# A two-layer graph network on one core: longer rests in the update chain, ten shared row buffers, full-array products and one activation table

## The chip, the cores and the metric

The kernel runs on one core of a Trainium2 chip. A core has engines that run side by side, each with its own stream of instructions: PE (TensorE, matrix products), DVE (VectorE), ACT (ScalarE), POOL (GpSimd) and SP (SyncE, which here only queues DMA transfers). They wait for one another through semaphores. The metric is the device time of one execution in microseconds (us). Three executions of the kernel before took 3070.16, 3073.55 and 3084.93 us; the median is 3073.55. One more execution was recorded by the hardware profiler, and took 3064.87 us.

## The reference

There are 6250 nodes with 256 features, and 106250 edges (50000 pairs in both directions and a loop at every node), sorted by destination. Each edge has one of two types. The first layer:

```python
msgs = zeros_like(S)                          # S = x[src]
for r in range(2):                            # edge_nn: two relu layers with the same weights
    msgs = where((rel == r)[:, None], edge_nn(S, W_rel[r], b_rel[r]), msgs)
agg = segment_sum(msgs, dst)
i, f, g, o = split(agg @ W_ih.T + b_ih + b_hh, 4)
c = sigmoid(i) * tanh(g);  hn = sigmoid(o) * tanh(c)
h = relu(hn @ W1.T + b1);  h = relu(h @ W2.T + b2);  out = h @ W3.T + b3
x = layernorm(x + out)
```

The second is an attention layer with four heads of 64 features, with a maximum over the edges that enter each node:

```python
h = (x @ W).reshape(n, 4, 64)
e = leaky_relu(a_src[src] + a_dst[dst], 0.2)  # a_src = sum(h * att_src), a_dst likewise
ex = exp(e - segment_max(e, dst)[dst])
alpha = ex / segment_sum(ex, dst)[dst]
o = segment_sum(h[src] * alpha[..., None], dst) + bias
y = relu(layernorm(o + x) * ln_gamma + ln_beta)
x = layernorm(x + y)
```

All data is float32.

## The kernel before

**Messages.** A message depends on the source node and the edge type alone, so the messages of all nodes are computed once for both types, split in three bfloat16 parts (768 numbers of 2 bytes a row), and written to the table `parts0` in DRAM. Beside it the kernel makes the indices of the rows that each edge needs (`idx0` for layer 0, `idx1` for layer 1), and for each edge the place of its destination in its window (`slot`).

**Tiles, windows, groups, pairs.** 128 edges are a tile; there are 831 tiles. Seven tiles are a window (119 windows), whose destinations lie in 64 consecutive nodes; the tile after the seventh may still hold edges of the window, so a window is summed over eight tiles (`tiles_of(w)[1]`), and a tile at a border is used by two windows. Two windows are a group of 128 node slots (60 groups), and two groups a pair, except the last four groups, which stand alone.

**The order of the work** is written by hand (`tc.manual_schedule()`): each engine runs its instructions in the order of the code. One loop over the tiles per layer issues one gather a step (L1057, an indirect DMA on POOL's queue that fetches 128 rows by index), then the matmuls that are due, and then `run.step()`. The class `Steps` (L1065) holds chains, written as generators: at each step every chain that is due runs on to its next `yield n`, and rests n steps. So a chain's stages are spread between the gathers and the sum's matmuls of later tiles.

**Layer 0.** Gathers go to 20 buffers of one tile (`g0`). Four steps (`LAG`) after its gather, a tile is added to its group's sum in PSUM by three matmuls, one for each bfloat16 part, with a one-hot matrix of the destinations as the stationary operand (`sum0`, L1337). When a group is full, the chain `turn` copies the sum (L1177) and transposes it on PE (L1181); when a pair is full, the chain `update` runs: the gates (L1214 on PE, L1222 on ACT, sigmoid and tanh), the cell (L1227 to L1233), three linear layers (L1237 to L1257), the residual and layernorm (L1260 to L1276), transposes (L1282), and the product with the attention weights (L1294). It writes the rows of layer 1 (264 numbers, of which 260 are stored) to `rows1` (L1304) and the values needed later to `kept`, and fills `node3`, which holds the node's part of the attention logits as three bfloat16 parts.

**Layer 1.** Gathers go to seven buffers of one window each (`G`, seven tiles). The chain `ahead` (L1406) loads the destinations of the pair's edges, makes a transposed one-hot matrix, and spreads the nodes' logits to the edges by small products (L1449: 64 rows, 8 columns, three parts summed in PSUM), copied by ACT at L1460. The chain `weights` (L1463) takes the segment maxima with scans along the edges and ends in `ex`, the exponentials; it waits in `while late` until the windows of the pair before have been taken up. `weighted` (L1514) makes a window's one-hot matrix and multiplies its gathered rows by `ex` (L1529, tile `gw`); the multiplication is the last use of the row buffer `G`. `sum1` (L1617) adds tile after tile to the group's sum (L1633, in float32). The chain `finish` (L1536) divides, adds the loop's part, and does both layernorms with Sqrt on ACT (L1576) and a reciprocal on DVE (L1580).

A gather into a buffer waits until the buffer's last reader is done: the sum's matmuls in layer 0, the multiplication into `gw` in layer 1. ACT holds one set of function tables at a time; where the next function is of another set, a table load (`ACT_TABLE_LOAD`) stands ahead of it.

Of the kernel before, what the change touches and what calls it, by code (L numbers as in the profile page):

```python
# [44 lines left out]
H = 4  # L45
# [652 lines left out]
def gnn_kernel(  # L698
# [66 lines left out]
    with (  # L765
# [15 lines left out]
        with (  # L781
# [110 lines left out]
            nc.vector.tensor_sub(slot[:, : NW - 1, WT], after, lows[:, : NW - 1])  # L892
# [99 lines left out]
def fast(  # L992
# [103 lines left out]

    iops = ctx.enter_context(tc.tile_pool(name="iops", bufs=1, space=PSUM))
    iota8 = iops.tile([P, WT + 1, SLOTS], F32, name="iota8")
    for j in range(WT + 1):
        nc.scalar.copy(iota8[:, j, :], iota_f[:, :SLOTS])  # L1100
    keep = ctx.enter_context(tc.tile_pool(name="keep", bufs=1))
    node3 = keep.tile([P, NG, 3, 2 * H], BF16, name="node3")
    loop = keep.tile([P, NG, H], F32, name="loop")
    eps_c = keep.tile([P, 1], F32, name="eps_c")
    nc.vector.memset(eps_c, EPS)
    ctx.enter_context(tc.manual_schedule())

    def one_hot(to, w, nj):
        nc.vector.tensor_tensor(  # L1109
            to[:, :nj, :],  # L1110
            iota8[:, :nj, :],
            slot[:, w, :nj, None].to_broadcast([P, nj, SLOTS]),
            op=OP.is_equal,
        )


    with (
# [31 lines left out]
        nc.sync.dma_start(W3T_s, W3T)  # L1149
        zero = l0w.tile([(NP + P - N) // 2, 2 * HA], F32, name="zero")  # L1150
# [20 lines left out]
        def turn(g, i, ps, aT):  # L1171
# [6 lines left out]
            yield 1  # L1178
# [9 lines left out]
        def update(groups, aT):  # L1188
            cols = len(groups) * P
# [11 lines left out]
            yield 2  # L1201
            hn = up.tile([P, 2, 2 * P], F32, name="fhn")
            cells = []
            for m in range(2):
                gate = {}
                for name, part, func in (
# [14 lines left out]
                    gate[name] = up.tile([P, 2 * P], F32, name="f" + name, bufs=4)  # L1221
# [3 lines left out]
                    yield 1  # L1225
                cell = gate["gg"][:, :cols]
                nc.vector.tensor_mul(cell, cell, gate["gi"][:, :cols])  # L1227
                cells.append((cell, gate["go"][:, :cols]))
            for m, (cell, go) in enumerate(cells):
                nc.scalar.activation(cell, cell, AF.Tanh)  # L1230
            yield 1
            for m, (cell, go) in enumerate(cells):
                nc.vector.tensor_mul(hn[:, m, :cols], cell, go)  # L1233
            yield 1
# [7 lines left out]
            yield 2  # L1242
# [4 lines left out]
            yield 2  # L1247
# [4 lines left out]
            for i, g in enumerate(groups):  # L1252
# [6 lines left out]
                nc.vector.tensor_add(xn[u, i, :], xn[u, i, :], b3r[u, :])  # L1259
# [4 lines left out]
                yield 1  # L1264
            r = rstd[:, : len(groups)]
            nc.scalar.activation(r, mv[:, : len(groups), 1], AF.Sqrt, bias=eps_c)
            yield 2
            nc.vector.reciprocal(r, r)
            for i, g in enumerate(groups):
# [5 lines left out]
            yield 1  # L1275
            hs = []  # L1276
# [12 lines left out]
            yield 1  # L1289
            for i, g in enumerate(groups):  # L1290
# [6 lines left out]
                hr = up.tile([P, D + 2 * H], F32, name="hr")  # L1297
                nc.scalar.copy(hr[u, :], ph[u, :])
                nc.scalar.copy(keep3[u, i, 2, :], ph[u, :D])
                yield 1  # L1300
                for w in windows_of(g):
# [3 lines left out]
                    else:  # L1305
# [5 lines left out]
                        )  # L1311
                nc.sync.dma_start(kept[g, u, :], keep3[u, i, :, :].rearrange("p c f -> p (c f)"))

                nd = up.tile([P, 2, H], F32, name="nd")
                left = up.tile([P, 2, H], F32, name="left")
                nc.vector.tensor_copy(nd[u, 0, :], hr[u, HA : HA + H])
# [3 lines left out]
                n3 = [node3[u, g, c, :].rearrange("p (a h) -> p a h", a=2) for c in range(3)]  # L1320
# [4 lines left out]
                nc.vector.tensor_sub(n3[2], left[u, :, :], n3[1])  # L1325

        got, ohs, sums, turned = {}, {}, {}, {}
# [25 lines left out]
        for t in range(EC + LAG):  # L1353
            if t < EC:
                got[t] = ep.tile([P, 3 * D], BF16, name="g0", bufs=20)
                gather(got[t], parts0, idx0[:, t : t + 1])
                if t % WT == 0:
                    w = t // WT
                    ohs[w] = ep.tile([P, WT + 1, SLOTS], BF16, name="oh0")
                    one_hot(ohs[w], w, len(tiles_of(w)[1]))  # L1360
# [9 lines left out]
    with (  # L1370
        tc.tile_pool(name="fl1", bufs=1) as l1,
# [6 lines left out]
        vec = l1.tile([P, 2, D], F32, name="fvec")  # L1378
        for k, v in enumerate((gamma, beta)):
            nc.sync.dma_start(vec[:, k, :], rows(v, D))  # L1380
        slot_p = l1.tile([P, 1], F32, name="slot_p")
# [362 lines left out]
```

## Time and profile before

| quantity | value |
|---|---|
| median of three executions | 3073.55 us |
| profiled execution | 3064.87 us |
| its span, first to last instruction | 3063.1 us |
| PE busy (x instructions) | 1868.3 us (61%), x9984 |
| DVE busy | 1256.6 us (41%), x3394 |
| ACT busy | 767.3 us (25%), x1829 |
| POOL busy | 1583.2 us (52%), x1674 |
| stages: start / layer-0 gathers / gap / layer-1 gathers / end | 196 / 1234 / 46 / 1501 / 86 us |
| gathers of layer 0 and of layer 1, L1057 | 831 and 831, 949 and 951 ns each |
| fps matmuls of layer 0, L1337 | 2847, 433.8 us |
| fps matmuls of layer 1, L1633 | 1898 records, 650.7 us |
| pn products, L1449 | 2847, 100.8 us |
| ACT table loads, L1576, L1548, L1222 | 60, 58 and 31, 1283 ns each |

How to read it: busy times are of instructions that do work; waits, branches and the issue of a transfer are not in them. A row of the profile such as "L1529 DVE TENSOR_TENSOR gw<-G,exE 128x1792 f32 x118" is a group of instructions by line, engine, operation and tiles. "[10.19 <-DVE gw L1529]" is idle time of the engine ahead of an instruction, and what ended it. "issue" is time for which the profile shows no wait. Granted clock is the TensorE clock that was allowed, as a share of the full one.

### The profile page before, as it was taken

Reading aid. Unit: us, or ns where it says so; the run is one execution under the profiler, and the core shown is the slowest. Engines: PE = TensorE matmul, PEld = TensorE weight load, DVE = VectorE, ACT = ScalarE, POOL = GpSimd, SP = SyncE. Lnnn points to the kernel's source line nnn. Section 1 sums busy time; section 2 is a strip of 40 time slices with the busy share of each in tenths; the row PEclk is TensorE's granted clock in tenths of the full one; section 3 lists DMA queues with packets and bytes.
Section 4 is the critical chain, followed back from the end, with each engine's and each line's share of the span. In section 5 each row is a group of like instructions: output and inputs, shape, how many; then the busy total and the mean of one; then the engine's idle time right before and its main releaser. Section 6 shows DMA issues by size and latency. Waiting matters only on the chain. (4 is left out here: it accounts for less than half of the span.)

```text
span 3063.1 us, 31458 instructions
## 1 busy us (share of the span) xinstructions
PE 1868.3 (61%) x9984; PEld 1092.3 (36%) x9984; DVE 1256.6 (41%) x3394; ACT 767.3 (25%) x1829; POOL 1583.2 (52%) x1674
## 2 busy tenths in 40 slices
PE   8956777776777676778145554545454545454544
PEld 5644444444444444445122222222222222222222
DVE  6531222222222222223135555554555454545556
ACT  5631222222222222223012222222222222222223
POOL 0036666666666666664545554555455545454540
PEclk9977778878878888888566666666666766666667
DMA  4455555555555555554423434343434343434331
GB/s 152 155 166 145 158 164 164 164 166 162 157 168 165 164 171 162 159 167 136 119 71 98 114 101 110 100 113 100 110 100 113 100 111 98 112 97 115 97 103 32
DMA packets 183539, 395.17 MB, mean 129 GB/s; under 512 B 51925, under 2 KB 91800, under 8 KB 183362
## 3 DMA queue, kind: packets, MB, share of 16 engines
q0 software_dynamic: 93168, 274.27, 32.9%
q1 hardware_dynamic: 88993, 118.00, 12.5%
q8 instruction: 80, 1.31, 0.2%
q10 hardware_dynamic: 1200, 0.79, 0.1%
q14 instruction: 98, 0.79, 0.1%
HBM read 333.63 MB, written 59.30 MB: 128 GB/s over the span
## 5 line engine op out<-in xcount | busy, mean ns | idle before, releaser
L1057 POOL DMA_INDIRECT G<-rows,fidx x831 | 790.1, 951 | 714.8 <-DVE gw L1529 463.0
L1057 POOL DMA_INDIRECT g<-parts,fidx x831 | 788.7, 949 | 638.4 <-DVE zero L1151 193.9
L1633 PE MATMUL fps<-gw,oh 128*64 128x264 f32 x1898 | 650.7, 502 | 248.1 <-DVE gw L1529 166.4
L1337 PE MATMUL fps<-g,oh 128*64 128x256 bf16 x2847 | 433.8, 311 | 69.8 <-DVE oh L1109 25.8
L1633 PEld LDWEIGHTS fps<-gw,oh 128*64 128x64 f32 x1898 | 294.2, 173 | 498.1 <-issue 371.0
L1337 PEld LDWEIGHTS <-oh 128*64 128x64 bf16 x2847 | 275.4, 121 | 248.2 <-issue 188.3
L1529 DVE TENSOR_TENSOR gw<-G,exE 128x1792 f32<-128x1792 f32 (+1 forms) x237 | 278.3, 1215 | 90.8 <-ACT gw L1521 75.6
L1214 PE MATMUL fpg<-faT,fWihT 128*128 128x256 f32 (+1 forms) x768 | 250.3, 456 | 71.8 <-issue 61.4
L1109 DVE TENSOR_TENSOR oh<-iota,fslot 128x512 bf16<-128x512 f32 (+1 forms) x238 | 161.7, 680 | 252.2 <-remote 120.5
L1449 PE MATMUL pn<-node,ohT 64*128 64x8 bf16 x2847 | 100.8, 166 | 234.6 <-issue 180.6
L1214 PEld LDWEIGHTS fpg<-faT,fWihT 128*128 128x128 f32 x768 | 151.5, 225 | 135.8 <-issue 102.3
L1449 PEld LDWEIGHTS <-ohT 64*128 64x128 bf16 x2847 | 70.9, 100 | 347.2 <-issue 337.0
L1471 PE MATMUL turn<-fident,e 128*128 128x128 f32 (+2 forms) x32 | 14.9, 465 | 247.6 <-issue 132.0
L1227 DVE TENSOR_TENSOR fgg<-fgg,fgi 128x256 f32<-128x256 f32 (+1 forms) x64 | 26.3, 410 | 292.7 <-issue 175.9
L1576 ACT ACTIVATE frs<-fmv,eps_c 128x1 f32<-128x1 f32 x120 | 35.4, 295 | 424.6 <-issue 173.6
L1460 ACT COPY of<-pn 128x64 f32<-128x64 f32 (+1 forms) x119 | 18.9, 210 | 396.7 <-remote 311.5
L1260 DVE TENSOR_TENSOR keep<-fpg,fxn 128x256 f32<-128x256 f32 (+1 forms) x60 | 25.4, 424 | 222.4 <-PE fps L1337 109.6
L1294 PE MATMUL fpg<-Wx,fyT 128*128 128x264 f32 (+1 forms) x240 | 93.3, 525 | 22.6 <-ACT fyT L1286 12.0
L1584 ACT ACTIVATE fy<-fy,frs 128x256 f32<-128x256 f32 x120 | 71.9, 600 | 121.7 <-DVE frs L1581 100.6
L1184 DVE COPY faT<-fpg 128x256 f32<-128x256 f32 x60 | 24.5, 409 | 182.5 <-remote 98.9
L1471 PEld LDWEIGHTS turn<-fident,e 128*128 128x128 f32 (+2 forms) x32 | 5.6, 174 | 261.7 <-issue 139.0
L934 PE MATMUL fph<-fxc,fWrT 128*128 128x512 f32 (+1 forms) x208 | 89.2, 578 | 0.6 <-ACT fhT L941 0.3
(178 smaller groups left out, 2166.4 us busy)
## 6 DMA issues: line engine op xcount, KB each, us to landing
kept<-keep SPq DMA_DIRECT2D x59, 384.0 KB
k<-kept SPq DMA_DIRECT2D x59, 384.0 KB
parts<-ms SPq DMA_DIRECT2D x49, 384.0 KB
g<-parts,fidx POOLq DMA_INDIRECT x831
G<-rows,fidx POOLq DMA_INDIRECT x831
dB<-slot_a SPq DMA_DIRECT2D x118, 112.0 KB
rows<-hr SPq DMA_DIRECT2D x118, 65.0 KB
fxn<-in_x_dram SPq DMA_DIRECT2D x118, 64.0 KB
```

Source lines behind the costliest of these rows:

```text
L934: nc.tensor.matmul(ph[:, :cols], WrT_s[:, r, k, m * P : (m + 1) * P], xc[:, k, :cols], start=(k == 0), stop=(k == 1),)
L1057: nc.gpsimd.indirect_dma_start(out=to_tile, out_offset=None, in_=table, in_offset=bass.IndirectOffsetOnAxis(ap=idx, axis=0), **more,)
L1109: nc.vector.tensor_tensor(to[:, :nj, :], iota8[:, :nj, :], slot[:, w, :nj, None].to_broadcast([P, nj, SLOTS]), op=OP.is_equal,)
L1214: nc.tensor.matmul(pg[:, :cols], WihT_s[:, k, c * P : (c + 1) * P], aT[:, k, :cols], start=(k == 0), stop=(k == 1),)
L1227: nc.vector.tensor_mul(cell, cell, gate["gi"][:, :cols])
L1294: nc.tensor.matmul(ph[u, :], hs[i][:, k, u], Wx[:, k, :], start=(k == 0), stop=(k == 1))
L1337: nc.tensor.matmul(sums[g][half_of(w), :], ohs[w][:, j, :], got[t][:, c * D : (c + 1) * D], start=(j == 0 and c == 0), stop=(t == tiles[-1 ...
L1449: nc.tensor.matmul(pns[w][:, j, :], ohT[half_of(w), j, :], node3[half_of(w), g, c, :], start=(c == 0), stop=(c == 2),)
L1529: nc.vector.tensor_mul(gw[:, j0 : j0 + jn, :D].rearrange("p j (h f) -> p j h f", h=H), of[:, :jn, :D].rearrange("p j (h f) -> p j h f", h= ...
L1576: nc.scalar.activation(rs[u, k, 0:1], mv[u, k, 1:2], AF.Sqrt, bias=eps_c[u])
L1584: nc.scalar.activation(y, y, AF.Identity, bias=m, scale=r)
L1633: nc.tensor.matmul(sums[g][half_of(w), :], oh[:, j, :], gw[:, j, :], start=(j == 0), stop=(j == n - 1))
```

## The change

- In layer 0 the rests between the stages of `update` grow from 1 or 2 steps to as many as 3 (`slow`, which is 3 for most pairs and 1 for the last). Four gate buffers become six, and `hr` gets five. The bias `b3` is added earlier. 
- Both layers take their row buffers from one pool of ten: four tiles to a buffer in layer 0 (40 tiles), one window to a buffer in layer 1 (70 tiles).
- The products in `ahead` use all 128 rows of the array: `node3` gets a padded half for each window of the group, so that one product for a tile gives both windows and all three parts (48 columns), and DVE sums the three parts. ACT copies the parts into the padded halves, two small copies for each group.
- In layer 1 a group has 15 places for tiles instead of twice 8: the tile that both of its windows share is weighted, looked up and summed once, with both one-hot matrices side by side. The one-hot matrices are made once for a group. For that, `slot` is -1 in a window's eighth tile unless the next window's first edge lies inside.
- `weights` no longer waits in `while late`; `ex` has two buffers, in a PSUM tile beside the one row of indices that all one-hot matrices now read. The chain has some longer rests.
- Layer 1 uses Ln and Exp, with a scale of -0.5, in place of Sqrt and reciprocal, and loads one table set that holds both ahead of the layer.
- `kept` rows are loaded when the group's sum opens and not when it closes; constants of layer 1 are loaded and made before layer 0; up to eight tiles are queued for `sum1` instead of six.

The core of the diff:

```diff
+    bank = iops.tile([P, SLOTS + 4 * GS * H], F32, name="bank")
+    iota_s = bank[:, :SLOTS]
+    exs = bank[:, SLOTS:].rearrange("p (b t h) -> p b t h", b=2, h=H)
-    node3 = keep.tile([P, NG, 3, 2 * H], BF16, name="node3")
+    node3 = keep.tile([P, NG, 2, 3, 2 * H], BF16, name="node3")
+    nc.vector.memset(node3, 0.0)
+    rowsp = ctx.enter_context(tc.tile_pool(name="rowsp", bufs=10))
...
         def update(groups, aT):
+            slow = min(3, max(1, (NG - 4 - groups[0]) // 4))
...
-            yield 2
+            yield 4
...
-                    gate[name] = up.tile([P, 2 * P], F32, name="f" + name, bufs=4)
+                    gate[name] = up.tile([P, 2 * P], F32, name="f" + name, bufs=6)
...
-                    yield 1
+                    yield (slow + 1) // 2
...
+            yield slow - 1
             for m, (cell, go) in enumerate(cells):
                 nc.scalar.activation(cell, cell, AF.Tanh)
-            yield 1
+            yield slow
             for m, (cell, go) in enumerate(cells):
                 nc.vector.tensor_mul(hn[:, m, :cols], cell, go)
-            yield 1
+            yield slow
...
+                yield slow
+                for s, w in enumerate(windows_of(g)):
+                    nc.scalar.copy(
+                        node3[half_of(w), g, s, :, :],
+                        nd3[half_of(w), :, :, :].rearrange("p c a h -> p c (a h)"),
+                    )
...
-                got[t] = ep.tile([P, 3 * D], BF16, name="g0", bufs=20)
+                if t % 4 == 0:
+                    four = rowsp.tile([P, 4, 3 * D], BF16, name="g0", tag="G")
+                got[t] = four[:, t % 4, :]
...
+        nc.scalar.preload_act_table_set("natural_log_exp_and_others")
...
-                for j in range(nj):
-                    for w in windows_of(g):
-                        for c in range(3):
-                            nc.tensor.matmul(
-                                pns[w][:, j, :],
-                                ohT[half_of(w), j, :],
-                                node3[half_of(w), g, c, :],
-                                start=(c == 0),
-                                stop=(c == 2),
-                            )
-                    if j % 2:
-                        yield 1
+                pn = ops.tile([P, 2, W8, 3, 2 * H], F32, name="pn", bufs=2)
+                for j in range(nj):
+                    nc.tensor.matmul(
+                        pn[:, :, j, :, :].rearrange("p s c a -> p s (c a)"),
+                        ohT[u, j, :],
+                        node3[u, g, :, :, :].rearrange("p s c a -> p s (c a)"),
+                        start=True,
+                        stop=True,
+                    )
+                yield 2
...
+                for o, parts in spans:
+                    nc.vector.tensor_reduce(
+                        of[:, o : o + parts.shape[1], :],
+                        parts.rearrange("p j c a -> p j a c"),
+                        axis=AX.X,
+                        op=OP.add,
+                    )
...
-            while late:
-                yield 1
-            ex = ops.tile([P, 4 * W8, H], F32, name="exE")
+            ex = exs[:, pairs.index(pair) % 2, :, :]
...
-                nc.scalar.activation(rs[u, k, 0:1], mv[u, k, 1:2], AF.Sqrt, bias=eps_c[u])
-                nc.vector.reciprocal(r, r)
+                nc.scalar.activation(r, mv[u, k, 1:2], AF.Ln, bias=eps_c[u])
+                nc.scalar.activation(r, r, AF.Exp, scale=-0.5)
+                yield 2
...
-            while late and len(queue) < 6:
+            while late and len(queue) < 8:
...
+                k3s[g] = fp.tile([P, 3, D], F32, name="k3")
+                nc.sync.dma_start(k3s[g][u, :, :].rearrange("p c f -> p (c f)"), kept[g, u, :])
...
+            if full and j == WT:
+                to, ohj = slice(0, P), ohs[g][:, WT : WT + 2, :].rearrange("p j s -> p (j s)")
...
-                    G[w] = ep.tile([P, WT, HA], F32, name="G", bufs=7)
+                    G[w] = rowsp.tile([P, WT, HA], F32, name="G", tag="G")
```

## The prediction

> **What bounds the kernel now.** I read the engine table by stages first, then the waits of POOL, then those of PE, and last the timeline around one long wait of POOL. The stages, with the seven columns length, PE, PEld, DVE, ACT, POOL busy, granted clock (then DMA share and GB/s):
>
> ```profile
> 0.00:196.00 196.00, 177.09 (x640) 116.89 (x640) 114.81 (x204) 122.77 (x216) 1.61 (x9) 0.99 0.42 146
> 196.00:1430.00 1234.00, 872.05 (x4224) 548.00 (x4224) 319.67 (x1112) 280.23 (x600) 788.74 (x831) 0.80 0.57 164
> 1430.00:1476.00 46.00, 33.58 (x183) 23.66 (x183) 19.47 (x84) 21.65 (x54) 1.83 (x2) 0.77 0.22 69
> 1476.00:2977.00 1501.00, 747.25 (x4750) 384.59 (x4750) 748.00 (x1837) 316.45 (x900) 789.99 (x831) 0.66 0.40 105
> 2977.00:3063.00 86.00, 38.32 (x187) 19.20 (x187) 54.65 (x159) 26.16 (x59) 1.08 (x2) 0.70 0.12 33
> ```
>
> The reader is to see two long stages of 831 gathers each, 1234 us (1.485 a gather) and 1501 us (1.806), in which no engine is full. A gather is 0.95 us of POOL and at least 0.30 of issue, so POOL alone would need 831 x 1.25 = 1039 us in each. What it waits for beyond that:
>
> ```profile
> POOL G L1057 <- DVE gw L1529: 463.0, 55, 20.9
> POOL G L1057 <- issue: 227.6, 747, 0.3
> POOL g L1057 <- PE fps L1337: 186.9, 221, 2.9
> POOL g L1057 <- issue: 142.8, 462, 1.9
> ```
>
> In layer 1 (tile G) it is 55 long waits, 463 us, for the weighting of an old row buffer: 1501 - 1039 = 462, the whole of the rest. In layer 0 (tile g) it is many short waits for the sum's matmuls: 1234 - 1039 = 195 us. So the kernel loses 657 us because row buffers come free late. Why late: PE's waits in layer 1 are led by
>
> ```profile
> PE pn L1449 <- issue: 180.6, 177, 11.6
> ```
>
> and the timeline of one pair of groups (start, length, engine, line, tiles, in brackets the idle time before) shows them:
>
> ```profile
> 1759.40 0.94 POOL L1057 DMA_INDIRECT G<-rows,fidx  x1 [10.19 <-DVE gw L1529]
> ...
> 1766.47 0.31 PE L1449 MATMUL pn<-node,ohT 64*128 64x8 bf16 x12
> ...
> 1769.35 0.22 PE L1449 MATMUL pn<-node,ohT 64*128 64x8 bf16 x3 [1.23 <-issue]
> ...
> 1771.45 0.21 PE L1449 MATMUL pn<-node,ohT 64*128 64x8 bf16 x3 [1.88 <-issue]
> 1772.88 0.16 PE L1449 MATMUL pn<-node,ohT 64*128 64x8 bf16 x1 [1.21 <-issue]
> ...
> 1779.59 0.33 ACT L1460 COPY of<-pn 128x64 f32<-128x64 f32 x2 [11.22 <-remote]
> ...
> 1782.33 0.94 POOL L1057 DMA_INDIRECT G<-rows,fidx  x1 [5.75 <-DVE gw L1529]
> ```
>
> Twelve small products take 0.31 us at 1766; from 1768 on they come singly, over 1 us apart, and the copy of the result on ACT has been idle 11.22 us. Then the ring of 7 buffers is empty and POOL stops. This repeats every pair (about 50.5 us = 28 gathers, 35 us, and stops of 10.2 and 5.75). PE has work but does not get on while gathers stream.
>
> **The change, part by part.** Durations are of the profiled execution, 3064.87 us (span 3063.1, 1.8 around it); the median of the runs, 3073.55, is 0.3% more.
>
> *Ten buffers (both layers).* Layer 1's ring goes from 49 gathers to 70, layer 0's from 20 to 40. Counted in the order of the code, a gather is issued 6 to 8 steps after its buffer's release before, some 25 after; 16 and some 33 in layer 0. 17 more gathers are 17 x 1.25 = 21 us of slack, against stops of 10.2, 5.75 and at most 20.9. Also POOL waits once per buffer (119 windows; every 4th gather in layer 0). Bounds: nothing kept of the 462 + 195 us, or all of it.
>
> *Products by the full array.* 2847 products of 64 rows and 8 columns become 477 of 128 rows and 48 columns; the sum over three parts moves to 178 DVE reduces in place of 119 ACT copies (119 x 0.21 = 25 us of ACT). PE: in a burst 12 products take 0.31 us; 100.8 us by the records. 477 x 0.17 to 0.31 (the 8-column product and the 256-column bf16 matmul of layer 0) = 81 to 148 us by records, so array time is about even: -20 to +47. DVE: 178 x 0.3 (128x128 tensor operations take 0.29) = 53 us more, bounds 0.18 to 0.43. What counts is `PE pn <- issue`, 180.6 us in 177 waits, a cost per instruction: with a sixth of the instructions, about 30.
>
> [...]
>
> *Shared tile once.* fps matmuls of L1633 949 to 890: 59 x 2 records x 0.50 = 59 us of PE; the one-tile weighting with 412 ns goes from 118 to 60: -24 us of DVE. One-hots are joined by group, the same elements.
>
> *Ln and Exp for Sqrt and reciprocal.* Removes 118 table loads in layer 1 (60 + 58, 1.283 us: 151 us of ACT), 120 reciprocals (19 us of DVE), adds 120 one-column activations (0.295: 35 us). In layer 0 the gates' loads go from 31 to 53, as stages of two pairs now mix: +28 us. ACT is busy 316 of 1501, so this is worth only latency: a finish chain loses two loads, 2.6 us. Taken at 0 for the sum; bounds 0 and -20. Cover: POOL.
>
> [...]
>
> *Rests in the update.* A chain of 22 steps becomes about 55 while a pair is 28 gathers, so two pairs' updates lie in each other. The work is the same. What it takes away are PE's waits between stages in layer 0: `fpg` rows of waits (L1214 61.4, L1181 44.9, L1282 39.1, L1237 32.5, L1244 30.0) are near 208 of some 290 us. With 3 steps (4 us) between stages, results that come 1 to 3 us late are there. Bounds: all 290, or none. PE busy 872 of 1130 would be 77%.
>
> *Moved or added waits.* kept rows are loaded when a group's sum opens, 15 or so steps before the finish: 21 waits, 52.9 us of DVE, go; SP only queues the load earlier (846 transfers become 787). Constants of layer 1 (vec, toward) move before layer 0: 4.4 us of POOL's wait in the gap. Zeroing node3 and three slot operations: under 3 us ahead of the first gather (DVE 115 of 196 busy, and POOL waits there for a chain of DVE): +2. Two small ACT copies a group (0.2 each, 24 us) beside gathers. `in_order` issues nothing.
>
> *Sum.* First stage 196. Layer 0: 831 x 1.36 = 1130; between 1.25 (POOL alone) and 1.485 (as now) I take the middle, since the ring doubles, but PE at 872 us busy leaves little slack. Gap 46 (the last updates have rest 1; bounds 40 to 65). Layer 1: 831 x 1.33 = 1105; nearer to 1.25 (1039) than to 1.806, since 21 us of slack exceeds each stop, DVE (748 + 53 - 24 - 19 = 758) and PE (747 - 59 - about 0) have room. Tail 100: 86 now, but up to 17 gathers more are waiting to be weighted at the last gather, some of it at double rate; bounds 75 to 130. 196 + 1130 + 46 + 1105 + 100 + 1.8 = 2579; on the scale of the median x 1.003 = 2587, say 2590.
>
> **Rivals.**
> B: layer 0 keeps its pace. For: PE gets on mainly when POOL pauses. If PE is fully busy in the 195 us of pauses, it has (872 - 195) / 1039 = 0.65 of its pace while gathers run, and 872 us of work then needs 1039 + (872 - 0.65 x 1039) = 1236 whatever the ring. Against: PE's waits are also of its own chain, which the rests take out. 2587 + 104 = 2690.
> C: layer 1 keeps part of its stops, as one pair's weights chain still stands between its last gather and the first release: half of 462 - 66, so 1105 + 165 = 1270: 2750. For: the chain has 4 more rests. Against: 25 steps of lead. B and C together 2855.
> D, the slower side: with POOL never stopping, PE's results are held back in all of both layers. Place: PE between gathers; price: with a share s of its pace under gathers, the two stages take 2 x 1039 + (872 + 688) - 2 x 1039 s. The start of layer 0 shows 30 sum matmuls (30 x 0.311 = 9.3 us) in 30 us, so s = 0.31: 2994, in all 3340. It decides against the change from s under 0.43 (the stages then take over 2740). Against: the mean s of layer 0 is 0.65.
> E: nothing to measure: buffers were not the cause and POOL waits elsewhere; the 463 us row speaks against it. 3075.
>
> **How the numbers follow.** Forecast 0.49, B 0.24, C 0.14, B with C 0.05, D 0.05, E 0.03. The time is the forecast's, 2590. The lower end is both stages at POOL's own pace and a tail of 75: 196 + 1039 + 46 + 1039 + 75 = 2395, say 2400. The upper end takes in B and C, and both together, 2850; D and E are left out, and about as much again for tails of the cases: under 2 in 10. Runs of this kernel differ by about 0.5%, and nearer than that is no change: faster 0.92 (the first four), same 0.02, slower 0.06 (D and part of E).
>
> **What would show it.** In the changed profile POOL's `gw` row should fall from 463 to under 100 us and the gathers be about 1.33 apart; in layer 0 the `fps` row of POOL should fall to about 90. `PE pn <- issue` should be 30, the layer-1 table loads none, ACT's copy of `of` gone. A `fps` row at 190 or more shows B; a `gw` row near 230 shows C, above all with waits that end on `ex` or `turn`; PE's waits on issue growing in both layers while POOL runs without stops shows D. The prediction is wrong most easily where PE, not the ring, sets layer 0's pace, or where the longer lead makes the tail much longer than 130.

## The result, and the profile after

The changed kernel took 3108.8 us (median of four, 3105.2 to 3112.3) against 3075.7 us for the kernel before: a ratio of 1.0104, with a 95% interval of 1.0076 to 1.0133. It is 1% slower, where 16% faster was forecast. The stages of the profiled execution (3109.83 us), in the columns of the table before:

```profile
0.00:196.00 196.00, 176.62 (x640) 116.80 (x640) 116.22 (x210) 121.25 (x209) 2.53 (x10) 0.99 0.43 148
196.00:1430.00 1234.00, 816.59 (x4082) 525.87 (x4083) 307.76 (x1075) 318.46 (x701) 784.33 (x828) 0.79 0.56 163
1430.00:1480.00 50.00, 46.84 (x305) 33.55 (x305) 22.53 (x88) 30.36 (x80) 4.37 (x5) 1.00 0.23 73
1480.00:3020.00 1540.00, 510.70 (x2290) 286.97 (x2291) 734.96 (x1845) 190.72 (x786) 795.36 (x832) 0.62 0.38 102
3020.00:3108.00 88.00, 42.32 (x183) 22.26 (x181) 64.44 (x182) 18.78 (x70) 0.94 (x1) 0.76 0.13 37
```

The reader is to see that PE is busy far less in the second long stage (511 us busy against 747) and ACT too (191 against 316), and that neither long stage is shorter. From first to last gather, layer 0 went from 1232 to 1240 us, layer 1 from 1500 to 1521; the time between the layers' gathers went from 48 to 62, the end from 87 to 90. POOL's waits:

```profile
POOL G L1064 <- DVE gw L1559: 488.5, 47, 36.2
...
POOL g L1064 <- PE fps L1385: 99.4, 50, 4.1
POOL g L1064 <- remote: 96.2, 38, 8.1
```

The row that should have fallen from 463 to under 100 stands at 488.5. The other engines' waits say where it comes from:

```profile
ACT ends L1525 <- PE turn L1524: 551.6, 31, 22.4
DVE s L1519 <- remote: 512.5, 26, 21.1
...
PE pn L1476 <- issue: 214.0, 105, 2.8
```

DVE's first scan of the chain `weights` waits some 20 us a pair. One pair in the timeline:

```profile
2038.15 0.47 PE L1512 MATMUL turn<-fident,e 128*120 128x128 f32 x1 [2.86 <-issue]
...
2042.16 0.46 PE L1476 MATMUL pn<-node,ohT 128*128 128x48 bf16 x7 [1.59 <-issue]
...
2055.40 0.94 POOL L1064 DMA_INDIRECT G<-rows,fidx  x1 [0.30 <-issue]
...
2061.88 0.42 DVE L1519 TENSOR_TENSOR_SCAN s<-cut,turn 120x128 f32<-120x128 f32 x1 [19.71 <-remote]
...
2073.60 2.02 DVE L1565 TENSOR_TENSOR gw<-G,bank 128x1792 f32<-128x1792 f32 x1
2073.62 0.95 POOL L1064 DMA_INDIRECT G<-rows,fidx  x1 [17.28 <-DVE gw L1559]
```

PE issues the transpose at 2038. The scan that needs it starts at 2061.88, 23.7 us later, and 6.5 us after POOL's last gather began. Then DVE works almost without a gap until the first row buffer is free at 2073.6. A pair is now one stream of 28 gathers (2021.4 to 2056.3) and one stop of 17.3 us, 52 us in all, where it was two stops of 10.2 and 5.75 us. The median from that transpose to its scan is 23.6 us over the 32 pairs and groups. The scan waits for one semaphore alone, PE's. In this stretch the trace has PE's steps of it at 2044.57, 2049.51, 2055.28 and 2060.29, some 5 us apart, and then eight within 0.32 us from 2061.78 on: the results of PE, and nothing that DVE or a load owes, are late.

In the kernel before, in the profile that the prediction reads, the same handover takes 0.51 us in the median. Its transpose comes about when POOL stops (1798.99, with a stop from 1799.6 on), and what is held there is the products, as the prediction's timeline shows. The change has moved the held stretch from the products to the head of the chain `weights`.

In the same stretches SP's instructions that only move a register or compute on one take some 0.70 us. Of 712 in the execution, 185 take over 0.3 us (158 in the kernel before); the median of all is 0.037.

### The profile page after: what moved, and what is told of

It reads as the page before. It is cut to its first block, busy times and chain, and to the rows that moved or that the text cites. A ratio compares the mean times of both kernels' runs of the same rounds, so it can differ in the third digit from the quotient of the medians.

```text
span 3108.0 us, 25949 instructions
## 1 busy us (share of the span) xinstructions
PE 1593.1 (51%) x7496; PEld 985.5 (32%) x7496; DVE 1245.9 (40%) x3397; ACT 679.6 (22%) x1845; POOL 1587.5 (51%) x1674
## 5 line engine op out<-in xcount | busy, mean ns | idle before, releaser
L1064 POOL DMA_INDIRECT G<-rows,fidx x831 | 794.4, 956 | 730.2 <-DVE gw L1559 488.5
L1064 POOL DMA_INDIRECT g<-parts,fidx x831 | 788.7, 949 | 645.4 <-issue 220.6
L1673 PE MATMUL fps<-gw,oh 128*64 128x264 f32 (+1 forms) x1780 | 453.6, 460 | 290.7 <-DVE gw L1559 200.1
L1673 PEld LDWEIGHTS fps<-gw,oh 128*64 128x64 f32 (+1 forms) x1780 | 241.9, 164 | 472.4 <-issue 357.4
L1565 DVE TENSOR_TENSOR gw<-G,bank 128x1792 f32<-128x1792 f32 (+1 forms) x178 | 264.8, 1488 | 69.8 <-ACT gw L1564 27.7
L1248 PE MATMUL fpg<-faT,fWihT 128*128 128x256 f32 (+1 forms) x768 | 228.7, 426 | 40.3 <-DVE faT L1217 26.3
L1523 PE MATMUL turn<-s,toward 120*120 120x1 f32 (+2 forms) x64 | 15.9, 317 | 342.9 <-DVE s L1520 339.6
L1476 PE MATMUL pn<-node,ohT 128*128 128x48 bf16 (+1 forms) x477 | 42.9, 211 | 228.9 <-issue 214.0
L1135 DVE TENSOR_TENSOR oh<-bank,fslot 128x512 bf16<-128x512 f32 (+1 forms) x179 | 153.1, 856 | 0.3 <-ACT bank L1543 0.3
L1295 PE MATMUL fpg<-fW3T,fz 128*128 128x256 f32 x120 | 62.9, 620 | 81.3 <-issue 61.6
L1476 PEld LDWEIGHTS <-ohT 128*128 128x128 bf16 (+1 forms) x477 | 26.7, 113 | 231.2 <-issue 216.3
L1214 PE MATMUL fpg<-fident,agg 128*128 128x128 f32 x120 | 31.5, 354 | 121.0 <-ACT agg L1210 83.0
```

The costliest lines, as they stand in the source:

```text
L1064: nc.gpsimd.indirect_dma_start(out=to_tile, out_offset=None, in_=table, in_offset=bass.IndirectOffsetOnAxis(ap=idx, axis=0), **more,)
L1135: nc.vector.tensor_tensor(to[:, :nj, :], iota_s[:, None, :].to_broadcast([P, nj, SLOTS]), of[:, :, None].to_broadcast([P, nj, SLOTS]), op= ...
L1214: nc.tensor.transpose(pt[:, k * P : (k + 1) * P], agg[:, k * P : (k + 1) * P], ident)
L1248: nc.tensor.matmul(pg[:, :cols], WihT_s[:, k, c * P : (c + 1) * P], aT[:, k, :cols], start=(k == 0), stop=(k == 1),)
L1295: nc.tensor.matmul(p3, z2[:, i * P : (i + 1) * P], W3T_s, start=True, stop=True)
L1476: nc.tensor.matmul(pn[:, :, j, :, :].rearrange("p s c a -> p s (c a)"), ohT[u, j, :], node3[u, g, :, :, :].rearrange("p s c a -> p s (c a) ...
```

## The experiments

The kernels ran on several chips, each time with the kernel before beside them. The chips turned out to be of two kinds: on the chip of the result and on chips A, D and F the kernel before takes 3031 to 3076 us, and the register instructions of SP are slowed as above; on chips B, C and E it takes 2475 to 2486 us, and none of the 712 takes over 0.3 us. I call the first the chips with the hold-up. Chip B was used twice and was of the same kind both times; none of the others from A to F came up again, so whether a kind belongs to a chip for good is not shown. From here on ratios are taken on one chip only. Which chip the result was taken on is not known, and the kernel before differs by 1.4% between chips with the hold-up, which is more than the 1% of the result. But on chip A the four altered forms of the changed kernel take 1.2 to 1.8% more than the kernel before, too. The unaltered changed kernel ran on the chip of the result and on chip C alone, and most kernels once on a chip.

**Chip A, with the hold-up (kernel before 3031.3).**

*PE's results not read in `ahead` and `weights`* (`still` is a constant tile; what read `pd` and `pm` reads a constant too):

```diff
-            nc.vector.tensor_tensor_scan(a, fore, pe[:rs, :], FAR, op0=OP.add, op1=OP.max)
+            nc.vector.tensor_tensor_scan(a, fore, ident[:rs, :], FAR, op0=OP.add, op1=OP.max)
...
+                pn = still
```

> The changed kernel, where the chains ahead and weights of layer 1 read constant tiles in place of what PE wrote for them (the four tiles pe, pd, pm and pn; PE still makes them), so that the segment maximum and the logits of the nodes are left out. Theory 1 (results of PE are held back while gathers stream, so the chain of weights gets on only in POOL's stops): the stops of 17 us a pair go, layer 1 falls from 1540 to 1050 to 1200 us, the whole to about 2650 to 2800. Theory 2 (the chain itself is long, by its rests and by DVE's order, whoever feeds it): under 100 us are won, 3000 or more.

Measured: 3076.5 us, layer 1 1499 from first to last gather. It does not tell the theories apart, because the chain still waited for PE: DVE overwrites `e`, which PE's transpose has to have read, and the wait is for PE's semaphore.

```profile
2044.50 0.28 DVE L1529 TENSOR_TENSOR e<-e,of 128x120 f32<-128x120 f32 x1 [18.79 <-PE turn L1527]
```

The step that goes on has moved from the scan to the next write; the wait is the same.

*No loads of `dB` and `cut` after the first pair:*

```diff
+            again = len(pair) == 2 and "dBs" in boxes[0]
+            if again:
+                cut, dBs = boxes[0]["cut"], boxes[0]["dBs"]
```

> The changed kernel, where the pairs of layer 1 after the first take over the first pair's dB and cut tiles in place of loading their own (so all pairs but the first and the single groups compute with wrong slots): about 630 of some 1150 packets a pair that SP's queue moves are left out. Theory 1a (the gathers alone hold PE's results back): layer 1 stays at 1480 or more, the whole above 3040. Theory 1b (it takes the burst of SP's loads on top of the gathers, which the trace shows just ahead of each slow stretch): layer 1 falls to 1100 to 1350, the whole to 2670 to 2920.

Measured: 3084.7 us, layer 1 1506, the transpose 23.1 us ahead of its scan. The bursts of SP's loads are not the cause.

*Seven row buffers:*

```diff
-    rowsp = ctx.enter_context(tc.tile_pool(name="rowsp", bufs=10))
+    rowsp = ctx.enter_context(tc.tile_pool(name="rowsp", bufs=7))
```

> The changed kernel with seven row buffers in place of ten (28 tiles in layer 0, 49 in layer 1). Theory 1 (a pair's stop is made of a drain and of the chain after it, and the ring only sets when it comes): layer 1 within 40 us of 1540, layer 0 within 30 us of 1234, the whole 3060 to 3160. Theory 3 (the ring's length still buys time): layer 1 longer by 100 us or more, above 3200.

Measured: 3066.5 us; layer 1 1510, layer 0 1226, between them 52. The other three kernels on chip A have ten buffers and take 1495 to 1506 in layer 1 and 1228 to 1235 in layer 0, so the ring's length buys nothing in either layer on this kind of chip.

*A small memset, 128x64, after each gather of layer 1:*

```diff
+                nc.gpsimd.memset(pad, 0.0)
```

> The changed kernel with one small memset on POOL (128x64) after every gather of layer 1, so that gathers come some 0.2 to 0.4 us further apart. If a stream without a pause is what holds PE's results back, the slow stretch shrinks, and although POOL has more to do, layer 1 falls below 1500 (28 gathers of 1.55 us make 43 us a pair against 52): 2800 to 3050. If pace does not matter, the 28 gathers just take longer ahead of the same stop of 17 us: layer 1 about 1540 + 831 x 0.3 = 1790, the whole about 3350.

Measured: 3076.8 us. The memset of 0.17 us hid in the 0.30 us of issue: most gathers came 1.28 us apart in place of 1.25. In each pair two or three came some 2 to 3 us apart, as POOL's memset waited:

```profile
POOL pad L1692 <- remote: 63.0, 56, 1.7
```

Outside the stops gathers so came 1.39 us apart in the mean, in place of 1.26 in the unaltered kernel. The stops (351 us for `gw` in place of 489) fell by about what that adds, and layer 1 took 1495. A gap that is 0.03 us longer moves the wait and ends nothing.

**Chip B, without the hold-up (kernel before 2485.8).**

*The logit of the node's own loop as the softmax's shift*, which takes PE, the scans and `cut` out of `weights`:

```diff
-            pe = tps.tile([P, P], F32, name="turn")
-            nc.tensor.transpose(pe[:rs, :], ef, ident)
...
-            nc.vector.tensor_tensor(by(top), by(pm[:, :rs]), aown, op=OP.max)
-            nc.vector.tensor_add(by(top), by(top), adst)
+            nc.vector.tensor_add(by(top), aown, adst)
```

> The changed kernel with the logit of the node's own loop as the shift of the softmax in place of the segment maximum (the softmax is the same in exact arithmetic): the chain weights loses its three results of PE, its four scans and the cut loads, and is DVE and ACT alone. Theory 1 (the chain gets on only in POOL's stops because PE's results are held back while gathers stream): the stops of 17 us a pair shrink to under 6, layer 1 falls to 1080 to 1300, the whole to 2620 to 2860. Theory 4 (DVE stands anyway, behind its waits for the pn products and for the sums, which stay in the kernel): layer 1 1350 to 1500, the whole 2900 to 3060.

*A memset of 128x512 after each gather of layer 1* (the edit of the smaller one, with 512 columns):

> The changed kernel with a memset of 128x512 on POOL after every gather of layer 1 (some 0.5 us, so that gathers are about 1.65 us apart; the smaller one of the run before hid in the gap of issue). If a gap between gathers lets PE's results through, the stops shrink from 17 to under 6 us a pair and layer 1 takes 1370 to 1500: 2930 to 3060. If only a stop of many us does, layer 1 takes 831 x 1.65 + 29 x 17 = 1860, the whole about 3400.

*Rests of one step in the update chain:*

```diff
-            slow = min(3, max(1, (NG - 4 - groups[0]) // 4))
+            slow = 1
```

> The changed kernel with the rests of the update chain of layer 0 undone (slow is 1 throughout; the first rest of 4 and the turn's 2 stay). If the longer rests gain in layer 0 what another part loses, layer 0 grows by 50 us or more over 1235; if results of PE come in bursts that no rest of 3 gathers outlasts, layer 0 stays within 25 us, and the gap behind it, 62 us with rests, gets no longer.

*Without the gates' matmuls:*

```diff
-                    pg = upp.tile([P, 2 * P], F32, name="fpg")
-                    for k in range(2):
-                        nc.tensor.matmul(pg[:, :cols], ...)
+                    pg = still
```

> The changed kernel without the gates' matmuls (768 of PE's, 229 us); ACT reads a constant tile in their place, so that the aggregated messages have no part in the result. If PE's throughput under the gathers bounds layer 0, it falls by about 229 x 0.8 = 180 us to 1050; if the waits of POOL in layer 0 come from late results of the sum's own matmuls, it falls by less than 60, to 1170 to 1230.

Measured: 2386.4, 2714.9, 2380.6 and 2387.5 us. Three of the four lie together: in both layers gathers are 1.25 to 1.27 us apart in the mean, and no two are over 3 us apart, whether the rests are 3 or 1, the gates are made or not, the maximum is taken or not. POOL's own pace sets all three; the paced one is POOL's longer pace, 1.67 us. The conditions that the expectations set were those of the other kind of chip, so these runs did not tell the theories apart. They showed that the chips differ.

**Chip C, without the hold-up (kernel before 2475.2): both kernels unaltered, and two of the variants again.**

> The changed kernel, unaltered, on the chip of this call. In the call before, on another chip than that of the result, the kernel before took 2486 us and three variants of the changed one 2381 to 2387. If the chips differ and not the variants, then on a chip where the kernel before takes near 2490 this one takes 2380 to 2400 with gathers 1.26 us apart in both layers, and on one where it takes near 3050 this one takes 3060 to 3110 with stops of 17 us a pair.

> The kernel before, unaltered, for its trace on this chip. Where it takes near 2490 us: gathers 1.25 to 1.27 us apart in layer 0, 1.30 to 1.45 in layer 1, and no instruction of SP that only moves a register takes 0.7 us. Where it takes near 3050: the stages of the profile before, within 40 us each.

> The changed kernel with the loop's logit as the shift of the softmax (no PE result, scan or cut load in the chain weights), on the chip of this call. Where the kernel before takes near 3050 us: by theory 1 (only PE's late results stop the chain) layer 1 falls from 1520 to 1080 to 1300 us, the whole to 2620 to 2860; by theory 4 (DVE stands anyway behind the pn products and the sums) the whole is 2900 to 3060. Where it takes near 2490: 2380 to 2390, as in the call before, since POOL sets the pace already.

> The changed kernel with a memset of 128x512 on POOL after every gather of layer 1 (gathers 1.67 us apart at least, measured in the call before), on the chip of this call. Where the kernel before takes near 3050 us: if a gap between gathers lets PE's results through, layer 1 takes 1390 to 1450 and the whole 2930 to 3020, less than the changed kernel; if not, stops of 10 us or more a pair come on top, layer 1 1700 or more, the whole above 3270. Where it takes near 2490: 2710 to 2720.

Measured: the changed kernel 2378.6 us against 2475.2, a ratio of 0.9606 with an interval of 0.9578 to 0.9634; the kernel before once more 2482.3; 2390.3 and 2709.3 for the two variants. **On this chip the change gains 4%.** Layers 0 and 1 of the changed kernel there:

```profile
196.00:1240.00 1044.00, 819.16 (x4307) 520.08 (x4307) 325.16 (x1143) 341.41 (x752) 790.60 (x830) 0.88 0.67 195
...
1273.00:2324.00 1051.00, 512.57 (x2363) 291.62 (x2364) 770.09 (x1889) 193.27 (x797) 797.80 (x831) 0.68 0.54 150
```

Each is 831 x 1.26 us. The handover that took 23.7 us is there at once, in the middle of the stream:

```profile
2021.72 0.47 PE L1512 MATMUL turn<-fident,e 128*120 128x128 f32 x1 [8.79 <-ACT e L1704]
2021.76 0.95 POOL L1064 DMA_INDIRECT G<-rows,fidx  x1 [0.30 <-issue]
2022.23 0.42 DVE L1519 TENSOR_TENSOR_SCAN s<-cut,turn 120x128 f32<-120x128 f32 x1
```

It takes 0.51 us in the median, against 23.6. The kernel before, on this chip:

```profile
1272.00:2399.00 1127.00, 632.12 (x4750) 341.37 (x4750) 749.03 (x1846) 315.79 (x904) 792.64 (x831) 0.73 0.52 140
```

```profile
POOL G L1057 <- DVE gw L1529: 83.8, 22, 6.4
```

So 84 of the 463 us of stops belong to the kernel; the rest came with the chip. With them went the products' waits: the row `PE pn <- issue`, 180.6 us in the prediction, does not occur here, and PE stands 13 us in all before the products, 11.9 of them once for a load. What the change gains: layer 1 1127 to 1051, and the end 81 to 54 us. Layer 0 is at POOL's pace in both (1043).

**Chip B again (kernel before 2484.6).**

*Parts of the gathers with different edits in one kernel:* the shift of `n_loop` in pairs 9 to 17, and memsets of 256 or 512 columns in parts of layer 0 (first lines) and of layer 1:

```diff
+                if 280 <= t < 560:
+                    nc.gpsimd.memset(pad[:, :256], 0.0)
...
+                if 18 * 28 <= t < 23 * 28:
+                    nc.gpsimd.memset(pad[:, :256], 0.0)
+                elif 23 * 28 <= t < 28 * 28:
+                    nc.gpsimd.memset(pad, 0.0)
```

> The changed kernel with other edits in parts of its gathers, to be read from the stages: layer 0 gathers 280 to 559 with a memset of 128x256 on POOL after each (gathers 1.43 us apart at least); layer 1 pairs 9 to 17 with the loop's logit as shift (no PE result in the chain weights); pairs 18 to 22 with the memset of 128x256, pairs 23 to 27 with 128x512 (1.66 us apart). Where the chip lets results through (kernel before near 2490 us): 1.26 us a gather in the plain parts and in pairs 9 to 17, 1.43 and 1.66 in the paced ones. Where it does not (kernel before near 3050): plain parts 1.48 in layer 0 and 1.82 in layer 1; by theory 1 pairs 9 to 17 need 1.25 to 1.45, by theory 4 1.65 or more; if a gap of 0.2 or 0.4 us lets results through, the paced parts show their own pace without stops (1.43, 1.66), else 1.6 or more in layer 0, 2.0 or more in layer 1.

Measured: 2519.5 us, each part at its own pace (1.26, 1.46, 1.26 in layer 0; 1.27, 1.26, 1.48, 1.67 in layer 1).

*The kernel before with a ring of ten in layer 1:*

```diff
-                    G[w] = ep.tile([P, WT, HA], F32, name="G", bufs=7)
+                    G[w] = ep.tile([P, WT, HA], F32, name="G", bufs=10)
```

> The kernel before with ten row buffers in layer 1 in place of seven, and nothing else. Where the kernel before takes near 2480 us (layer 1 1127, 22 stops for gw): if the ring is the part that brings the gain, layer 1 falls to 1050 to 1070, the whole by 60 to 80 us; if the shorter chain is (products, table loads, shared tile), it stays above 1100. Where it takes near 3050: layer 1 within 30 us of 1500.

Measured: 2484.6 us, no change. Layer 1's gathers take 23 us less (1104 us, against 1127 on chip C), and the end grows from 81 to 108. The stops return with about the same size:

```profile
POOL G L1057 <- DVE gw L1529: 62.3, 18, 5.1
```

The first two gathers over 3 us apart come at 1818 us in place of 1509, and from there such places are 39 us apart: the consumer needs about 39 us a pair and POOL 35, so a longer ring puts off the stops and does not end them. The ring alone so brings none of the 4%, and the consumer's shorter work is what is left; the changed kernel with seven buffers was not run on such a chip. Which of the products, the shared tile, the table loads or the earlier `kept` loads brings how much was not separated.

**Chip D, with the hold-up (kernel before 3030.8): the mixed kernel again.**

> The kernel of the run mixed, on the chip of this call, for the kind of chip on which the result was taken. Where the kernel before takes near 2490 us: as in the run mixed, 2510 to 2530. Where it takes near 3050: plain parts 1.48 us a gather in layer 0 and 1.82 in layer 1; by theory 1 (only PE's late results in the chain of weights stop it) pairs 9 to 17 need 1.25 to 1.45, by theory 4 (DVE stands anyway behind the pn products and the sums) 1.65 or more; if a gap of 0.2 or 0.4 us between gathers lets results through, the paced parts show their own pace without stops (1.43, 1.66), else 1.6 or more in layer 0, 2.0 or more in layer 1.

Measured: 2965.7 us, 2.1% less than the kernel before, from the parts:

| part | us a gather, with hold-up (D) | without (B) |
|---|---|---|
| layer 0, plain, first and last third | 1.464 and 1.482 | 1.257 and 1.257 |
| layer 0, memset of 256 columns | 1.463, no two over 3 us apart | 1.455 |
| layer 1, plain, pairs 3 to 9 | 1.953; 1.856 after the first stop of 36 us | 1.272 |
| layer 1, loop's logit (gathers of pairs 11 to 17) | 1.744 | 1.265 |
| layer 1, 256 columns, last four of five pairs | 1.481, no two over 3.2 us apart | 1.484, the same |
| layer 1, 512 columns, last four of five pairs | 1.674, no stop | 1.668 |

Two answers. First, theory 4 against theory 1: without any PE result in `weights`, the stops are still about 14 us a pair, where they were 17. DVE stands elsewhere, ahead of the same work. The timeline of such a pair:

```profile
2129.86 0.95 POOL L1064 DMA_INDIRECT G<-rows,fidx  x1 [0.30 <-issue]
2135.56 0.16 DVE L1592 TENSOR_TENSOR sm<-loop,fps 128x4 f32<-128x4 f32 x1 [8.70 <-remote]
...
2139.33 0.28 DVE L1516 TENSOR_TENSOR e<-e,of 128x120 f32<-128x120 f32 x1
...
2144.91 0.95 POOL L1064 DMA_INDIRECT G<-rows,fidx  x1 [14.11 <-DVE gw L1571]
```

DVE waits for PE's sum in `finish` until 5.7 us after the last gather starts; the chain's steps stand behind that in DVE's order. Second, with a gap some 0.2 us longer after each gather the stops are gone in these parts of one execution, in both layers; in layer 0 the pace stays what it was with them. POOL's waits over pairs 23 to 27 hold nothing but its own issue:

```profile
POOL G L1064 <- issue: 17.5, 106, 0.2
```

**Chips E and F: a whole kernel so paced, the changed one with a memset of 128x256 after each gather of layer 1.**

> The changed kernel with a memset of 128x256 on POOL after every gather of layer 1, nothing else. Where the kernel before takes near 3050 us: layer 1 831 x 1.48 = 1230 in place of 1520, the whole 2790 to 2850, 6 to 9% less than the kernel before. Where it takes near 2480: layer 1 1230 in place of 1051, the whole 2540 to 2580, 2 to 4% more than the kernel before.

> The changed kernel with memsets of other lengths on POOL after the gathers, to be read by parts: layer 0 gathers 0 to 279 with 96 columns, 280 to 559 with 160, the rest with 208; layer 1 pairs 0 to 6 with 96, 7 to 13 with 160, 14 to 20 with 208, the rest with 256; their own paces are about 1.31, 1.36, 1.41 and 1.46 us. Where the chip holds results up, I expect stops of POOL in the parts with 96 and 160 (1.46 or more a gather in layer 0, 1.7 or more in layer 1) and none with 256; 208 is open. Where it does not: each part at its own pace.

Chip E is without the hold-up: 2538.2 us against 2484.8, a ratio of 1.0221 (1.0203 to 1.0239), and 2582.7 us for the scan of gaps, each part at its own pace. From which gap on the hold-up ends stays open.

> The kernel of the run pace_l1 (a memset of 128x256 on POOL after every gather of layer 1), on the chip of this call. Where the kernel before takes near 3050 us: layer 1 831 x 1.48 = 1230 in place of 1520, without stops, the whole 2790 to 2850, 6 to 9% less than the kernel before. Where it takes near 2480: as in the call before, 2530 to 2545, 2.2% more.

Chip F has the hold-up: **2909.2 us against 3073.8, a ratio of 0.9443 (0.9378 to 0.9508).** There, one added memset a gather makes the kernel 5.6% faster than the kernel before, while the changed kernel was 1% slower on the chip of the result. The layer took 1317 us, not 1230, against 1214 on chip E:

```profile
1501.00:2818.00 1317.00, 502.02 (x2288) 283.98 (x2289) 743.62 (x1820) 185.14 (x771) 1078.54 (x1661) 0.63 0.44 119
```

```profile
POOL G L1064 <- DVE gw L1560: 100.6, 13, 11.7
```

13 waits of 101 us are left where the changed kernel had 47 of 489 on its chip, and 13 of the 32 scans still come 10 to 25 us after their transposes. On chip D, too, scans in the part with 256 columns came up to 12 us late, though without a stop. So this gap weakens the hold-up and does not end it.

## Why the prediction was wrong

*The bound.* "The kernel loses 657 us because row buffers come free late" was read rightly from the two long stages, and the cause of the lateness was not. Without the hold-up the kernel before loses 84 us of it in layer 1 and nothing in layer 0, which is why even there the change gains 4% and not 16%. Some 585 us of 3065 came with the hold-up (3064.9 against 2475 to 2482), which the change does not touch.

*Ten buffers.* This is the step that failed first. I set 21 us of slack against stops of up to 20.9 and concluded that most of the 462 us go; the `gw` row rose to 488.5. The sum holds for a delay that comes now and then. Here the delay comes with every pair: results are held back until POOL stops, so POOL runs until the ring is empty, however long it is. Seven buffers gave the same layer 1 (1510 us) as ten in the other runs on chip A (1495 to 1506). And without the hold-up the ring alone gave nothing either.

*Products by the full array.* "A cost per instruction: with a sixth of the instructions, about 30" was wrong. The row went from 180.6 us in 177 waits to 214.0 in 105, and on chip C it does not occur in either kernel: it was not the products that cost so much each, but PE was held at that time. The reading was off, too: in the lines shown the products come in threes, a tile's three parts, and not singly. On array time, the products' busy time went from 100.8 to 42.6 us on the chip of the result and from 71 to 29 on chip C, more than the bounds of -20 to +47 allowed. What joining the two halves and joining the three parts brought each was not measured, as one product does both. With all parts together PE's busy time in layer 1 fell by 236 us (by 120 on chip C), where the sum had 59, and the layer got no shorter. The DVE price was near: 178 reduces took 45 us in place of 53.

*Table loads* went as counted (one left in layer 1, 53 in the gates). That they are worth nothing on the path was an estimate, and no run shows it by itself.

*Rests in the update.* "With 3 steps (4 us) between stages, results that come 1 to 3 us late are there": rests are counted in gathers, and what was late was late for as long as gathers stream. POOL's `fps` row fell to 99.4 us, near the 90 that was to show success, but with a wait only once in four gathers the time turned up in other rows (`remote` 62.2 to 96.2, `issue` 142.8 to 220.6). Layer 0 stayed at 1.49 us a gather; where nothing is held up, rests of 1 and 3 give the same 1042 to 1043 us.

*Sum.* Layer 0 1130 and layer 1 1105 lay between two values, and the chip has one or the other: 1240 and 1521 with the hold-up, 1043 and 1051 without. Rival B's layer 0 (1236) came within 4 us, but by its making: the formula gives back 1039 + 195, the time before, whatever PE does. PE's throughput is not what set that pace, since on chip C layer 0 takes 1043 with the same work. Rival D named the mechanism, results held back in both layers, and was given 0.05 at 3340 us. Its price was off in both layers (1589 and 1405 us, where 1240 and 1521 came), and its share of 0.31 rests on a miscount: the first 30 us of gathers hold 54 sum matmuls and not 30. I had weighed the held-up PE as something the ring could cover, though the timeline shown in the prediction said that PE's work ends only when POOL stops. That line should have led.

*What is not settled.* Which resource is held up. Shown: it is strongest with gathers 1.25 to 1.28 us apart (waits for `gw` of 489 us on the chip of the result and 351 on chip A), weaker at 1.45 to 1.48 (101 us on chip F), and all but gone in the five pairs at 1.67 (2 of 48 register instructions over 0.3 us); in the pair above it is there 17 us after a stream begins (2021.4 to 2038.15), in the prediction's pair 9 us (1759.40 to 1768); it delays PE's results (23.6 us from transpose to scan) and slows SP's register instructions, these to some 0.70 us each; it ends some 5 us after the last gather (2056.3 to 2061.78); SP's loads of `dB` and `cut` do not bring it on (23.1 us without them); and some chips do not have it (0.51 us on chip C). A handover from DVE to ACT early in the stretch above took 0.03 us (2039.95 to 2039.98), but none falls in the rest of it. Two causes do not fit. The granted clock of layer 1 is lower with the hold-up (0.62 against 0.68 for the changed kernel), but PE is busy for 511 and 513 us, so there its work is not slower. And the packets of POOL's gathers take 161 ns in the median on both kinds of chip. Every time of the experiments comes with a span and a granted clock, so it is of a recorded execution; whether one without records is held up was not tried.

## What to carry to other kernels

A stop that comes once in every period, at the same place, is a rate and not a jitter. Here a longer ring moved it (with ten buffers, without the hold-up, the first stop came at 1818 us in place of 1509, and the stops stayed 39 us apart), and the change, whose consumer has less work, removed it (84 us of stops in the kernel before on chip C, no wait for `gw` over 0.3 us in the changed one). Look at how long a result takes from the engine that makes it to the one that waits, and at trivial instructions that take far longer than their kind: where both grow together, as here (23.6 us in place of 0.51 for the transpose, and 0.70 for register instructions with a median of 0.037), the delay may not be in the kernel's order, and one should measure on another chip before pricing anything against it. With the hold-up a gap some 0.2 us longer after each gather cost less than the stops (5.6% faster than the kernel before on chip F), and where nothing was held back it cost its full length (layer 1 1214 us on chip E, 1051 without the gap on chip C).

## What the runs showed of the hardware

- The kernel before takes 2475 to 2486 us on some chips and 3031 to 3076 on others (22 to 24% more), and the change gains 3.9% on one of the first kind and loses 1.0% on one of the second.
- On the second kind, with gathers 1.25 us apart, the changed kernel's transpose reaches DVE 23.6 us after its start in the median (0.51 on the first kind), and 158 to 217 of 712 register instructions of SP take over 0.3 us, most of them some 0.70 (0.037 in the median of all).
- There, gathers of layer 1 with a memset of 0.33 us on POOL after each need 1.48 us (four pairs, one execution) to 1.59 us (the whole layer) where back-to-back ones need 1.83 on the chip of the result.
